# A graph layer's last octets: an addition put ahead of the node statistics, a store cut in two, an earlier flag, and columns copied two octets longer

## The chip, the cores and the metric

The kernel runs on one core of one Trainium2 chip. A core has five engines that work side by side, each on its own queue: TensorE (PE, with its weight loads shown apart as PEld), VectorE (DVE), ScalarE (ACT), GpSimd (POOL) and SyncE (SP). They wait for each other through semaphores; DMA engines move data meanwhile. The metric is the device time of one execution in microseconds (us). A profile is a record of one execution; its span runs from the program's first instruction to its last.

## What is computed

A message passing layer on a graph with 12500 nodes of 64 features and 400000 edges with 16 features, the edges sorted by their destination:

```python
m_in = jnp.concatenate([x[src], x[dst], edge_attr], axis=-1)
h = jax.nn.silu(m_in @ W1 + b1)
messages = jax.nn.silu(h @ W2 + b2)
agg = jax.ops.segment_sum(messages, dst, num_segments=x.shape[0])
node_in = jnp.concatenate([x, agg], axis=-1)
x = _layernorm(x + jax.nn.silu(node_in @ W3 + b3), axis=-1)
```

## The kernel before

The edges are cut into 3125 tiles of 128, and the tiles into 391 **octets** of eight tiles (the last, number 390, has five). A loop over `o` (L759) handles one octet per step, in an order of instructions that is written out by hand for PE, ACT, DVE and SP (`manual_schedule`, L754). POOL runs its own list.

**Where source rows come from.** For most tiles POOL gathers 128 rows of a table with one indirect DMA (`gather`, L448). Some pairs of tiles are built another way, so that POOL issues two gathers fewer per pair: `columns` (L336 to L370) copies 128 columns of a transposed copy of the nodes, one small instruction per column, either on ACT (L367) or on DVE (L369), spread over the three or four octets before the one that uses them. Each group of 16 columns comes after loads of 32 addresses into registers. Which octets get such a pair is planned ahead in `pairs` (L327 to L332): the plan goes over `range(len(octs) - QUIET - 2)` and gives an octet `o + 2` a pair each time an engine has had room for 256 more edges. With `QUIET = 5` ACT builds 113 pairs (14464 columns) and DVE 125 (16000), the last of them used in octets 385 and 383. A third way, rows fetched singly by SP (L397), is not touched.

**One octet.** PE transposes the gathered rows into PSUM (L550), adds the products of copied columns (L553) and of the window and attributes (L554); ACT applies SiLU (L557, `h`); PE multiplies by W2 (L566, L568, `second_layer`); ACT applies SiLU (L572, `m`); PE sums the messages per destination (L581, `add_up`) into one of four places of the PSUM tile `sums`; DVE adds that window to `agg` (L592, `add_window`). [...] The steps at which these happen come from `times` (L727): over the last eight octets (`DRAIN`) `second_layer` is done one step after an octet's first layer, `add_up` two and `add_window` three steps after.

**Nodes.** 25 groups of 512 nodes (the last has 212, on 53 partitions of four nodes) are finished as soon as their sums are complete: products with W3 (L624, L630), SiLU (L636), the sum with x (L642), mean and variance (L647, L648), a square root (L651) and reciprocal (L654) for several groups at once, the division (L660), and the store (L664). The last two groups, `rest` and `rest + 1`, are done at the end.

**The end, in the order of the code.** In the last step but two of the loop's body (`o == NO - 1`, octet 390): `behind` (`add_up(388)`, `second_layer(389)`), the products, SiLU and statistics of group `rest` (L822 to L827), then `limits` (L701 to L718), twelve DVE instructions that check the input's shape, then octet 390's first layer. In step 391 `add_window(388)` comes first (L801), then `add_up(389)` and `second_layer(390)`; in step 392 `add_window(389)` and `add_up(390)`; after the loop `add_window(390)` (L879), the sums and statistics of the last group (L881 to L886), `verdict` (L720 to L725: a small product, a reduction and a conversion, which leave the flag in `badi`), the root, and for both groups division and store (L888 to L893).

**The flag.** After all of this every engine loads the flag `badi` into a register (L106) and branches (L108): if an input's shape is unusual, a general version of the layer is run, else the branch leads past its code. Behind it come semaphore updates that stand in for the part left out (recorded on L108), and the program's end (recorded on L1148): SP waits for all semaphores, each engine drains, and POOL, which gathers the engines' reports, releases them.

Of the kernel before, what the change touches and what calls it, by code (L numbers as in the profile page):

```python
# [20 lines left out]
P = 128  # L21
G = 4
# [19 lines left out]
HALF = 6144  # L42
OVER = 304
TURN = 195
QUIET = 5
DRAIN = 8
LAG = CT * P // 32
AHEADS = 256
# [6 lines left out]
@with_exitstack  # L55
def kernel(
    ctx: ExitStack,
    tc: tile.TileContext,
    x: bass.AP,
    xt: bass.AP,  # L60
    xt2: bass.AP,
    src_c: bass.AP,
    src_row: bass.AP,
    src_pair: bass.AP,
    dst_c: bass.AP,
    dst_row: bass.AP,
    attr_t: bass.AP,
    attr_2: bass.AP,
    base: bass.AP,
    w1: bass.AP,  # L70
    b1: bass.AP,
    w2: bass.AP,
    b2: bass.AP,
    w3: bass.AP,
    b3: bass.AP,
    out: bass.AP,
    edges: int,
):

    nc = tc.nc
    N, D = x.shape

    const = ctx.enter_context(tc.tile_pool(name="const", bufs=1))
    dram = ctx.enter_context(tc.tile_pool(name="dram", bufs=1, space=DRAM))
    pa = dram.tile([N, D], F32, name="pa")
    badi = const.tile([1, 1], I32, name="badi")
    ident = const.tile([P, P], F32, name="ident")
    make_identity(nc, ident)
    identb = const.tile([P, P], BF16, name="identb")  # L100
    nc.vector.tensor_copy(identb, ident)

    with ExitStack() as inner:
        windows(inner, tc, ident, identb, badi, pa, x, xt, xt2, src_c, src_row, src_pair, dst_c, dst_row, attr_t, attr_2, base, w1, b1, w2, b2, w3, b3, out, edges)

    flag = nc.values_load(badi[0:1, 0:1], min_val=0, max_val=4 * P,  # L106
                          skip_runtime_bounds_check_because="a count of partitions")
    with tc.If(flag > 0):  # L108
        general(tc, ident, x, xt, src_c, dst_c, dst_row, attr_t, w1, b1, w2, b2, w3, b3, out, edges)


def windows(ctx, tc, ident, identb, badi, pa, x, xt, xt2, src_c, src_row, src_pair, dst_c, dst_row, attr_t, attr_2, base, w1, b1, w2, b2, w3, b3, out, edges):
    nc = tc.nc
# [4 lines left out]
    NO = base.shape[1]  # L118
# [176 lines left out]
    with tc.tile_pool(name="gat", bufs=AHEAD + 2) as gat, \  # L295
# [32 lines left out]
        for eng in counts:  # L328
            pairs[eng] = []
            for o in range(len(octs) - QUIET - 2):  # L330
                if counts[eng][o] >= 2 * P * (len(pairs[eng]) + 1):
# [121 lines left out]
        def bases(eng, o):  # L453

            n = min(4, NO - o)
            at, least, most = (bi8, 0, 8 * (N - 1)) if eng == ENG.SP else (bi, AADDR, AADDR + 4 * (NA - S))
            _, regs = nc.values_load_multi_w_load_instructions(
                at[0:1, o:o + n], engines=(eng,), min_val=least, max_val=most,
                skip_runtime_bounds_check_because="dst names a node")
            for i in range(n):  # L460
                winreg[eng, o + i] = regs[i]
# [98 lines left out]
        def second_layer(o):  # L560
            c, t0, n, first, last = octs[o]
            n2 = n + n % 2
            k = n2 // 2
            h, eh = made.pop(o)
            p2 = ps2.tile([P, OT, D], F32, name="p2")
            nc.tensor.matmul(p2[:, :n2, :], one3, b2r[:, :n2, :], start=True, stop=False, skip_group_check=True)  # L566
            for i in range(k):
                nc.tensor.matmul(p2[:, 2 * i:2 * i + 2, :].rearrange("p s d -> p (s d)"), h[:, i, :], w2d,  # L568
                                 start=False, stop=(i == k - 1), skip_group_check=True)
            columns(o + 1, ENG.Activation, 1)  # L570
            m = msg.tile([P, OT, D], F32, name="m")
            nc.scalar.activation(m[:, :n2], p2[:, :n2], AF.Silu)  # L572
            made[o] = m, eh

        def add_up(o):
            c, t0, n, first, last = octs[o]
            m, eh = made.pop(o)
            pg = sums[:, o % 4, :]
            for i in range(n):
                s = i % 2  # L580
                nc.tensor.matmul(pg[s * D:(s + 1) * D, :], m[:, i, :], eh[:, i // 2, :, s],  # L581
                                 start=(i < 2), stop=(i >= n - 2), skip_group_check=True)
# [4 lines left out]
        def add_window(o):  # L587
            if o == TURN:
                nc.vector.tensor_copy(agg[:, :OVER], agg[:, HALF:HALF + OVER])
                clear(HALF, NA)  # L590
            a = agg.bitcast(U8)[:, ds((winreg.pop((ENG.DVE, o)) - AADDR).with_bounds(min_val=0, max_val=4 * (NA - S), guaranteed_mod_val=0, out_of_modulus=4), 4 * S)].bitcast(F32)
            nc.vector.tensor_tensor(a, a, sums[:, o % 4, :], op=OP.add)  # L592
# [4 lines left out]
        NG = len(groups)  # L597
        RB = 5
        v = nv.tile([P, 2 * RB, G, D], F32, name="v")
# [26 lines left out]
        def node_sums(q, i):  # L626
            c, n = groups[q]
            a = c if c < HALF else c - HALF
            av = agg[:, a:a + n].rearrange("k (p i) -> k i p", i=G)
            nc.tensor.matmul(nodes[q]["acc"][:n // G, i, :], av[:, i], w3s, start=False, stop=(i == G - 1),  # L630
                             skip_group_check=True)

        def node_silu(q):
            p = groups[q][1] // G
            z = nx.tile([P, G, D], F32, name="z")
            nc.scalar.activation(z[:p], nodes[q]["acc"][:p], AF.Silu)  # L636
            nodes[q]["z"] = z

        def node_add(q):
            p = groups[q][1] // G  # L640
            of = nodes.pop(q)
            nc.vector.tensor_add(v[:p, q % (2 * RB)], of["xa"][:p], of["z"][:p])  # L642

        def node_stats(q, i):
            p = groups[q][1] // G
            st = nx.tile([P, 6], F32, name="st")
            nc.vector.bn_stats(st[:p], v[:p, q % (2 * RB), i, :])  # L647
            nc.vector.bn_aggr(mv[:p, q * G + i, :], st[:p])  # L648
# [7 lines left out]
        def divide(q, i):  # L656
            p = groups[q][1] // G
            vi = v[:p, q % (2 * RB), i, :]
            j = q * G + i
            nc.vector.tensor_scalar(vi, vi, mv[:p, j, 0:1], rstd[:p, j:j + 1], op0=OP.subtract, op1=OP.mult)  # L660

        def store(q):
            c, n = groups[q]
            nc.sync.dma_start(out[c:c + n, :].rearrange("(p i) d -> p i d", i=G), v[:n // G, q % (2 * RB)])  # L664

# [11 lines left out]
        for q in range(rest):  # L679
            o = lead[due[q]] + LAST - 1  # L680
# [10 lines left out]
        for q0, q1 in batches:  # L691
            o = lead[due[q1 - 1]] + LAST + 2 * G
# [27 lines left out]
        def verdict(bad):  # L720
            pc = mis.tile([1, 4], F32, name="mm")
            nc.tensor.matmul(pc, onec, bad, start=True, stop=True)
            bs = nv.tile([1, 1], F32, name="bs")
            nc.vector.tensor_reduce(bs, pc, AX.X, OP.add)
            nc.vector.tensor_copy(badi, bs)  # L725

        def times(lags):  # L727

            at = {}
            for o in range(NO):  # L730
                at.setdefault(o + lags.get(NO - 1 - o, lags[None]), []).append(o)
            return at
# [3 lines left out]
        folds = times({None: LAST, **{k: 3 for k in range(DRAIN)}})  # L736
# [17 lines left out]
        with tc.manual_schedule(engines={ENG.PE, ENG.Activation, ENG.DVE, ENG.SP}):  # L754
# [4 lines left out]
            for o in range(NO + 2):  # L759
# [3 lines left out]
                for k in range(0, NA, XC)[3 * o - 3:3 * o] if o else []:  # L763
                    n = min(XC, NA - k)
# [33 lines left out]
                for b in range(0, NO, 4):  # L798
                    if o == b + (4 if b < NO - DRAIN else 2):
                        bases(ENG.DVE, b)  # L800
                for q in folds.get(o, []):  # L801
                    add_window(q)
                if o == 1:
                    relative(0, CT, SCT)
                for k in range(3 * o - 3, 3 * o) if 1 <= o < 6 else []:
                    if k < 2 * len(parts):
                        c = parts[k // 2]
# [5 lines left out]
                def behind():  # L813
                    for q in adds.get(o, []):
                        add_up(q)
                    for q in seconds.get(o, []):
                        second_layer(q)

                if o == NO - 1:
                    assert NG == rest + 2 and groups[rest][0] + groups[rest][1] + LAG <= (NO - 4) // (CT // OT) * STEP  # L820
                    behind()
                    for i in range(G):  # L822
                        node_sums(rest, i)
                    node_silu(rest)
                    node_add(rest)
                    for i in range(G):
                        node_stats(rest, i)  # L827
                    bad = limits()
# [42 lines left out]
                if o in (NO - 4, NO - 3):  # L871
                    q = rest + (o == NO - 3)
# [4 lines left out]
            for i in range(NO + 2, NO + LAST):  # L877
                for q in folds.get(i, []):
                    add_window(q)  # L879
            assert NO not in todo  # L880
            for i in range(G):  # L881
                node_sums(rest + 1, i)
            node_silu(rest + 1)
            node_add(rest + 1)
            for i in range(G):
                node_stats(rest + 1, i)  # L886
            verdict(bad)
            root(rest, NG)  # L888
            inverse(rest, NG)
            for q in range(rest, NG):  # L890
                for i in range(G):
                    divide(q, i)
                store(q)  # L893


@with_exitstack
# [255 lines left out]
```

## Time and profile before

| | |
|---|---|
| median of 3 runs | 3294.95 us (3292.81 to 3297.97) |
| the profiled execution's own time | 3292.35 us |
| its span | 3290.6 us |
| POOL busy | 2465.6 us (75%), 2505 gathers of L448 from the table and 94 from x |
| ACT busy | 3109.2 us (94%) |
| PE busy | 2486.1 us (76%) |
| DVE busy | 2042.4 us (62%) |
| mean granted TensorE clock | 0.708 |

The profiled execution's time lies 1.75 us above its span. In the rows of the profile a number in front of a unit's name is a time in us; "x16" counts instructions; what stands in brackets or behind a bar is the engine's idle time before the instruction and what ended it. The chain of waits follows the run backwards from its last compute instruction, always to what released it. "issue" means that nothing visible was waited for. The letter q behind an engine (POOLq) marks its sequencer, which waits, branches and issues DMAs.

### The profile page before, as it was taken

Reading aid. Unit: us, or ns where it says so; the run is one execution under the profiler, and the core shown is the slowest. Engines: PE = TensorE matmul, PEld = TensorE weight load, DVE = VectorE, ACT = ScalarE, POOL = GpSimd, SP = SyncE. Lnnn points to the kernel's source line nnn. Section 1 sums busy time; section 2 is a strip of 40 time slices with the busy share of each in tenths; the row PEclk is TensorE's granted clock in tenths of the full one; section 3 lists DMA queues with packets and bytes.
Section 4 is the critical chain, followed back from the end, with each engine's and each line's share of the span. In section 5 each row is a group of like instructions: output and inputs, shape, how many; then the busy total and the mean of one; then the engine's idle time right before and its main releaser. Section 6 shows DMA issues by size and latency. Waiting matters only on the chain. (4 is left out here: it accounts for less than half of the span.)

```text
span 3290.6 us, 88339 instructions
## 1 busy us (share of the span) xinstructions
PE 2486.1 (76%) x15344; PEld 1705.0 (52%) x15344; DVE 2042.4 (62%) x18296; ACT 3109.2 (94%) x15306; POOL 2465.6 (75%) x2607
## 2 busy tenths in 40 slices
PE   7867777777777777767777777777877867777786
PEld 5545555555555545544454554545545545554554
DVE  5566666666666666666666666666666666666652
ACT  2799999999999999999999999999999999999991
POOL 7777777777777777777777777777777777777774
PEclk8787777777667677677767767766666676667666
DMA  7222222222222222221221222222222222222221
GB/s 148 50 41 40 43 41 40 43 41 40 45 44 44 42 42 40 41 43 38 48 46 39 43 41 40 43 43 43 45 41 42 40 44 41 43 44 45 39 42 33
DMA packets 160868, 147.82 MB, mean 45 GB/s; under 512 B 103748, under 2 KB 113718, under 8 KB 159526
## 3 DMA queue, kind: packets, MB, share of 16 engines
q0 software_dynamic: 83168, 85.33, 14.6%
q1 hardware_dynamic: 62624, 47.00, 5.7%
q10 hardware_dynamic: 14502, 9.75, 1.4%
q14 instruction: 447, 3.66, 0.4%
q8 instruction: 127, 2.08, 0.3%
HBM read 135.44 MB, written 6.40 MB: 43 GB/s over the span
## 5 line engine op out<-in xcount | busy, mean ns | idle before, releaser
L448 POOL DMA_INDIRECT ga<-pa,sc x2505 | 2375.6, 948 | 763.9 <-issue 666.0
L367 ACT ACTIVATE cx<-xs,x 128x1 f32 x14464 | 2789.5, 328 | 24.9 <-issue 19.5
L369 DVE TENSOR_TENSOR cx<-xs,x 128x4 uint8 x16000 | 1288.9, 154 | 1095.6 <-issue 1073.7
L581 PEld LDWEIGHTS pg<-eh,m 128*64 128x64 f32 x6250 | 296.8, 184 | 674.5 <-DVE agg L592 344.5
L550 PE MATMUL p<-ident,ga 128*128 128x128 f32 x1253 | 347.1, 364 | 393.7 <-DMA ga<-pa,sc 392.6
L568 PEld LDWEIGHTS p<-w2d,h 128*128 128x128 f32 x3126 | 536.7, 259 | 186.5 <-issue 186.5
L568 PE MATMUL p<-w2d,h 128*128 128x128 f32 x3126 | 632.5, 365 | 0.0
L554 PE MATMUL p<-oh,xw 128*128 128x512 f32 (+1 forms) x758 | 584.6, 866 | 0.0
L581 PE MATMUL pg<-eh,m 128*64 128x48 f32 x6250 | 352.8, 271 | 211.4 <-DVE agg L592 209.1
L550 PEld LDWEIGHTS p<-ident,ga 128*128 128x128 f32 x1253 | 220.4, 186 | 468.4 <-issue 433.2
L557 ACT ACTIVATE h<-p 128x512 f32<-128x512 f32 x391 | 243.1, 622 | 53.5 <-PE p L554 33.1
L515 PE MATMUL ph<-identb,eh 128*96 128x128 bf16 x1563 | 211.9, 276 | 99.9 <-DVE oh L525 96.4
L572 ACT ACTIVATE m<-p 128x512 f32<-128x512 f32 x391 | 242.6, 620 | 41.6 <-PE p L568 40.0
L525 DVE COPY oh<-ph 96x512 f32<-96x512 f32 x391 | 263.1, 673 | 1.9 <-PE ph L515 1.9
L515 PEld LDWEIGHTS <-eh 128*96 128x96 bf16 x1563 | 163.4, 163 | 136.5 <-DVE oh L525 122.4
L566 PE MATMUL p<-b2r,one 3*128 3x512 bf16 x391 | 193.3, 494 | 53.7 <-ACT m L572 53.2
L472 PE MATMUL mm<-w1bb,xr 65*96 65x128 f32 x782 | 221.5, 377 | 6.6 <-DMA xr<-in_xt 4.0
L497 DVE TENSOR_TENSOR eh<-wrow,dc 128x384 f32<-128x384 f32 x392 | 212.5, 542 | 11.3 <-PE wrow L624 6.9
L554 PEld LDWEIGHTS p<-oh,xw 128*128 128x128 f32 x758 | 175.8, 284 | 0.0
L472 PEld LDWEIGHTS mm<-w1bb,xr 65*96 65x96 f32 x782 | 139.9, 230 | 8.1 <-DMA xr<-in_xt 4.2
L553 PE MATMUL p<-cx,w1d 128*128 128x128 f32 x474 | 122.1, 368 | 0.0
L477 DVE TENSOR_TENSOR xw<-mm,mask 96x128 f32<-96x128 f32 x391 | 108.1, 276 | 20.6 <-PE mm L472 18.0
(106 smaller groups left out, 980.1 us busy)
## 6 DMA issues: line engine op xcount, KB each, us to landing
rx<-pa SPq DMA_DIRECT2D x6400, 0.2 KB
ga<-pa,sc POOLq DMA_INDIRECT x2505
oh<-in_attr SPq DMA_DIRECT2D x130, 192.0 KB
xr<-in_xt SPq DMA_DIRECT2D x391, 24.0 KB
cxi<-in_src_pair SPq DMA_DIRECT2D x238, 1.0 KB
xs<-in_xt ACTq DMA_DIRECT2D x6, 512.0 KB
pa<-v ACTq DMA_DIRECT2D x12, 256.0 KB
x<-in_xt ACTq DMA_DIRECT2D x6, 512.0 KB
```

The source lines that it names most:

```text
L367: nc.scalar.activation(cols[key][:, k:k + 1], word(i, xb, XADDR), AF.Identity, bias=word(i + 4, x2b, X2ADDR))
L369: nc.vector.tensor_tensor(t[:, 4 * k:4 * k + 4], at(i, xb, XADDR), at(i + 4, x2b, X2ADDR), op=OP.max)
L448: nc.gpsimd.indirect_dma_start(out=ga[:, i, :], out_offset=None, in_=x if o < RAW else pa[:, :], in_offset=bass.IndirectOffsetOnAxis(ap=sc ...
L472: nc.tensor.matmul(pw[:E, :], winrow[o], w1bb.rearrange("k s m -> k (s m)"), start=True, stop=True)
L515: nc.tensor.matmul(ph[:E, i, :], eh[:, i, :, 1], identb, start=(i == 0), stop=(i == k - 1), skip_group_check=True)
L525: nc.vector.tensor_copy(oh[:E, :], ph[:E, :(n + 1) // 2].rearrange("p i e -> p (i e)"))
L550: nc.tensor.matmul(p1[:, i, :], g2.rearrange("p s d -> p (s d)"), ident, is_transpose=True, start=(i == c), stop=False, skip_group_check=True)
L554: nc.tensor.matmul(p1[:, :k], xw[o % 3], oh, start=False, stop=True, skip_group_check=True)
L557: nc.scalar.activation(h[:, :k], p1[:, :k], AF.Silu)
L568: nc.tensor.matmul(p2[:, 2 * i:2 * i + 2, :].rearrange("p s d -> p (s d)"), h[:, i, :], w2d, start=False, stop=(i == k - 1), skip_group_ch ...
L572: nc.scalar.activation(m[:, :n2], p2[:, :n2], AF.Silu)
L581: nc.tensor.matmul(pg[s * D:(s + 1) * D, :], m[:, i, :], eh[:, i // 2, :, s], start=(i < 2), stop=(i >= n - 2), skip_group_check=True)
```

## The change

It has five parts.

1. `QUIET` goes from 5 to 3, so that the plan covers two more octets. DVE gets one more pair, its 126th, used in octet 386 and copied in the steps 381 to 383; octet 386 has six gathers in place of eight. ACT's pairs stay as they are.
2. `add_window(388)` is taken from the head of step 391 to step 390, between `behind` and the products of group `rest`.
3. `verdict` goes ahead of the last group's sums and statistics.
4. The store of a group is cut at the last multiple of 16 partitions: the last group's 53 partitions go out as 48 and 5. Other groups have 128 and keep one store.
5. The flag is loaded inside `windows`, after the last group's divisions and ahead of its store, and returned.

```diff
-QUIET = 5
+QUIET = 3
...
     with ExitStack() as inner:
-        windows(inner, tc, ident, identb, badi, pa, x, xt, xt2, src_c, src_row, src_pair, dst_c, dst_row, attr_t, attr_2, base, w1, b1, w2, b2, w3, b3, out, edges)
-
-    flag = nc.values_load(badi[0:1, 0:1], min_val=0, max_val=4 * P,
-                          skip_runtime_bounds_check_because="a count of partitions")
+        flag = windows(inner, tc, ident, identb, badi, pa, x, xt, xt2, src_c, src_row, src_pair, dst_c, dst_row, attr_t, attr_2, base, w1, b1, w2, b2, w3, b3, out, edges)
+
...
         def store(q):
             c, n = groups[q]
-            nc.sync.dma_start(out[c:c + n, :].rearrange("(p i) d -> p i d", i=G), v[:n // G, q % (2 * RB)])
+            to, p = out[c:c + n, :].rearrange("(p i) d -> p i d", i=G), n // G
+            for a, b in ((0, p // 16 * 16), (p // 16 * 16, p)):
+                if b > a:
+                    nc.sync.dma_start(to[a:b], v[a:b, q % (2 * RB)])
...
-                for q in folds.get(o, []):
+                for q in folds.get(o, []) if o != NO else []:
                     add_window(q)
...
                     behind()
+                    for q in folds[NO]:
+                        add_window(q)
                     for i in range(G):
                         node_sums(rest, i)
...
             assert NO not in todo
+            verdict(bad)
             for i in range(G):
                 node_sums(rest + 1, i)
...
                 node_stats(rest + 1, i)
-            verdict(bad)
             root(rest, NG)
             inverse(rest, NG)
             for q in range(rest, NG):
                 for i in range(G):
                     divide(q, i)
+                if q == NG - 1:
+                    flag = nc.values_load(badi[0:1, 0:1], min_val=0, max_val=4 * P,
+                                          skip_runtime_bounds_check_because="a count of partitions")
                 store(q)
+    return flag
```

## The prediction

> **What bounds the kernel now.** I read the page first, then the timeline around octets 387 to 390, the chain of waits, and last the control instructions after the last compute.
>
> ```profile
> span 3290.6 us, 88339 instructions
> L448 POOL DMA_INDIRECT ga<-pa,sc x2505 | 2375.6, 948 | 763.9 <-issue 666.0
> ```
> ```profile
> 3238.73 0.45 PE L550 MATMUL p<-ident,ga 128*128 128x128 f32 x1 [1.93 <-DMA ga<-pa,sc]
> 3256.14 0.30 PE L550 MATMUL p<-ident,ga 128*128 128x128 f32 x1 [1.12 <-DMA ga<-pa,sc]
> 3259.87 0.94 POOL L448 DMA_INDIRECT ga<-pa,sc  x1 [0.30 <-issue]
> ```
>
> A gather and its pause take (2375.6 + 763.9) / 2505 = 1.25 us, and the pauses are nearly all POOL's own ("issue"): POOL gathers without a stop until 3260.8. Near the end PE waits for gathers, 1.93 us in octet 387 and 1.12 us in octet 389. So until octet 389's last gather lands POOL bounds the time. Then the bound moves. The chain of waits:
>
> ```profile
> 3264.39 0.43 DVE v L642
> ...
> 3268.74 0.12 DVE agg L592
> 3268.86 0.14 issue
> 3269.00 1.10 PE pg L581 x16
> 3270.09 0.43 PE p L566
> 3270.52 1.59 PE p L568 x6
> 3272.20 0.50 ACT m L572
> 3272.74 0.89 PE pg L581 x10
> 3273.65 0.21 DVE agg L592
> 3273.91 1.12 PE mm L630 x8
> 3275.05 0.39 ACT z L636
> ```
>
> From 3264.39 to 3268.74 it runs through DVE: the sum, the statistics of group rest and the limits, all queued ahead of the addition at 3268.74 (L592, window 388). Only then may PE add up octet 389, and everything behind it follows in a row. The chain ends with the divisions; the rest of the span is control, which I read by line and engine:
>
> ```profile
> 3277.37 0.14 DVE L725 CAST badi<-bs 1x1 int32<-1x1 f32 x1
> ```
> ```profile
> L106 POOLq TENSOR_LOAD <-badi x1: 511/511/511, 3277.5 to 3277.5; - x1
> ```
> ```profile
> L108 POOLq EVENT_SEMAPHORE  x5: 17/43/43, 3281.3 to 3284.2; - x5
> L108 POOLq COMPARE_BRANCH  x1: 53/53/53, 3278.1 to 3278.1; - x1
> L108 POOLq INC_SWDGE_SEM  x1: 1210/1210/1210, 3284.2 to 3284.2; - x1
> ```
> ```profile
> L1148 POOLq DRAIN  x3: 40/107/4230, 3285.5 to 3290.3; - x3
> ```
> ```profile
> SPq L1148 <- PEq L1148: 4.2, 2, 3.7
> SPq L1148 <- DMA ga<-pa,sc: 1.2, 1, 1.2
> ```
>
> POOL loads the flag the moment it is written (3277.51), branches at 3278.1, gets its next instruction at 3281.3, raises its semaphores until 3285.5 and drains for 4.23 us, to 3289.7; at 3290.6 all is over. SP, the last engine beside it, waits 1.2 us for POOL's semaphores and then 3.7 us until POOL lets it go. So the end hangs on POOL's flag: 3290.6 - 3277.5 = 13.1 us from the flag to the end.
>
> **The change part by part.** *Columns.* Two gathers go from octet 386: 2 x 1.25 = **-2.5 us** at POOL. Octets 387 and 389 are gather bound, with PE waiting 1.93 and 1.12 us, so the shift reaches octet 389 whole. The price is 128 copies on DVE in steps 381 to 383:
>
> ```profile
> L369 DVE TENSOR_TENSOR cx<-xs,x 128x4 uint8 x137 | 11.1, 155 | 9.9 <-issue 9.7
> ```
> ```profile
> 3156.00:3181.00 25.00, 20.08 (x136) 14.72 (x134) 15.44 (x150) 25.00 (x126) 18.87 (x20) 0.73 0.20 39
> 3181.00:3206.00 25.00, 16.00 (x98) 9.90 (x98) 6.69 (x30) 21.09 (x102) 18.88 (x20) 0.68 0.20 39
> 3206.00:3256.00 50.00, 40.54 (x262) 28.64 (x261) 12.74 (x46) 10.04 (x15) 37.75 (x40) 0.68 0.22 46
> ```
>
> The first row is the stretch 3156 to 3181: 137 copies take 11.1 us and 9.9 us of pauses for the register loads, 0.153 us each, so 128 take **19.6 us** of DVE's queue. The window rows give the busy time of PE, PEld, DVE, ACT and POOL in this order. In 3181 to 3206, where those steps lie, DVE is busy 6.7 of 25 us: 18.3 are free, and 1.3 us stick out. Behind them stand DVE's `add_window`, `compare_nodes` and `turned`, for which PE waits. A bound from below is 0, from above 19.6 us. I take 0, because the stretch before, 15.44 us of work and 9.9 of pauses on DVE, is just as full and POOL works as steadily in it, and because PE is idle for 50 - 40.54 = 9.5 us between 3206 and 3256, which swallows a lag of 1.3 us. The pair also takes one small index load on SP, one address operation on DVE, and a product (L553) in place of a transpose (L550): nothing of that is on a late path.
>
> *The addition.* It goes ahead of the sum of group rest, into this pause:
>
> ```profile
> 3264.39 0.42 DVE L642 TENSOR_TENSOR v<-xa,z 128x256 f32<-128x256 f32 x1 [6.24 <-ACT z L636]
> ```
> ```profile
> 3260.05 0.67 PE L581 MATMUL pg<-eh,m 128*64 128x48 f32 x16 [0.75 <-ACT m L572]
> 3264.96 0.49 ACT L557 ACTIVATE h<-p 128x384 f32<-128x384 f32 x1 [0.60 <-PE p L554]
> 3269.00 1.10 PE L581 MATMUL pg<-eh,m 128*64 128x48 f32 x16 [4.07 <-DVE agg L592]
> ```
>
> Its input is summed at 3260.72 and DVE is idle for 6.24 us until 3264.39, so the addition itself costs nothing; without that pause it would cost its 0.2 us. What is queued behind it, the sum L642, waits for ACT's z anyway. The products of group rest read `agg` and now wait for it, but they start behind `second_layer(389)`. The 4.07 us wait goes: `add_up(389)` and `second_layer(390)` run under the limits. At the chain's lengths they need h at 3265.45, then 1.59 + 0.1 + 0.50, done by some 3267.7. What is late next is DVE again: `add_window(389)` comes behind the limits, where 388 stood, at 3268.74; then `add_up(390)` starts at 3269.0 in place of 3272.74. **-3.7 us** for all that follows.
>
> *Verdict and flag.* The verdict's product, reduction and conversion now lie between `add_window(390)` (3273.65) and the last group's z (3275.44 at its end), where DVE idles. The addition's 0.21, a reduction and a conversion of 0.14 each and a tenth of waiting make 0.6 us, so the flag is written some 0.6 us behind the start of that addition, not 3277.51 - 3273.65 = 3.86. POOL has nothing else left and loads it at once: **-3.3 us** for POOL's 13.1 us, if these are of fixed length. Their parts (load, branch, semaphores, drain) name no partner in the trace, so I take the length as fixed; if the drain's end hangs on SP, the gain is smaller (rival B).
>
> *Who is last then?* The root, divisions, stores and SP's control shift by the first two terms only.
>
> ```profile
> 3278.91 1.13 SPq L664 DMA_DIRECT2D out<-v  x2
> ```
> ```profile
> L1148 SPq DRAIN  x3: 7/7/13, 3286.2 to 3290.0; - x3
> ```
>
> Without its 1.2 us wait SP would report at 3286.2 - 1.2 = 3285.0, and POOL's release takes 0.9 us more: 3285.9 in the old frame, against POOL's 3290.6 - 3.3 = 3287.3. POOL stays last by 1.4 us. So SP's flag load ahead of the last store and the second store instruction cost nothing: together some 0.4 us more or less on SP, under that 1.4 us. If the cover goes, they cost just that. ACT, DVE and PE load the flag where their lists end, as before. By the same cover the split store brings nothing, although its data land sooner:
>
> ```profile
> GB/s 0 0 0 33 66 66 4 274 180 20 33 25 74 12 49 37 53 25 25 86 25 16 0 0 33 0 33 0 0 0 0 0 0 0 0 0 0 0 0 0
> ```
>
> This is 3278 to 3288 in slices of 0.25 us: the first store passes at 274 and 180 GB/s, the last trickles at about 25 GB/s until some 3283.5. [...]
>
> *Sum.* -2.5 - 3.7 - 3.3 = **-9.5 us**. The span goes from 3290.6 to 3281.1, the profiled execution's own time from 3292.35 to 3282.9. That execution is 2.6 us below the median of 3294.95, so against the median I get **3285.4**.
>
> **The rivals.** *B: POOL's long drain waits for the others.* It ends 3.5 us behind SP's report (3286.2 to 3289.7). Against it: POOL started it before SP had reported. Then SP's chain decides: 3285.0 + 3.5 + 0.9 = 3289.4, less 6.2: -7.4 us, 3287.5.
>
> *C: the tail on half a clock.*
>
> ```profile
> 3243.00:3253.00 10.00, 10.00 (x55) 7.79 (x54) 2.71 (x11) 1.19 (x2) 7.56 (x9) 0.57 0.16 26
> 3253.00:3260.00 7.00, 5.19 (x46) 3.44 (x44) 1.65 (x6) 1.79 (x3) 5.17 (x7) 1.00 0.25 64
> ```
> ```profile
> 3242.38 2.08 PE L568 MATMUL p<-w2d,h 128*128 128x128 f32 x8
> 3260.97 1.16 PE L568 MATMUL p<-w2d,h 128*128 128x128 f32 x8
> ```
>
> The granted clock was 0.57 up to 3253 and 1.00 behind it, just before the tail's chain, and eight products of L568 take 2.08 us on the low clock, 1.16 on the full. If the rise comes later against the work, two such blocks cost 0.9 each, two of L581 0.4 each, and the other products of that chain, slowed in the same ratio, by estimate 1.7 together: +4.3, so -5.2 us, 3289.8. For it: the moved gathers shift the work against the clock's steps. Against it: PE is as busy before the tail as it was. [...]
>
> *D: the extra copies eat the gathers' gain.* DVE's 1.3 us grows, PE reaches octet 389 2.5 us late: -7.0, 3287.9. For it: DVE and ACT are full in the stretch before.
>
> *E, slower: the copies gate PE.* If next to none of the 19.6 us on DVE is hidden, PE falls back by that in steps 381 to 383, regains its 9.5 us of idle time and starts octet 389's tail 10.1 us later than now; the other terms give back 7.0: +3.1, **3298.0**. It decides from 16.5 us of exposed copies on. Against it: 18.3 us of free DVE time.
>
> That the change does not do what it says would show as a flag that POOL does not load sooner; that is -6.2 and lies between D and C.
>
> **How the numbers follow.** Forecast 0.52, B 0.16, C 0.15, D 0.12, E 0.05. Runs of before spread by 2.6 us around their median, and SP's bound alone would allow 1.4 us more gain. The range goes from 3285.4 - 1.4 - 2.6 = 3281.4 up to C with 1.5 us of that spread, 3291.3; E and the edges, some 0.15, stay out. 0.2% is 6.6 us, about what a measurement of this kernel can tell from no change. Faster by more: the forecast nearly whole (0.48) and two thirds of B and D (0.19), so 0.67; same: their rest, and C, 0.28; slower: E, 0.05.
>
> **What would show it.** Right: 2503 gathers on L448 and the last one 2.5 us sooner; 16128 copies on L369; no wait of PE L581 for DVE L592 near 4 us; `add_up(390)` right behind the limits; the flag's conversion about 0.6 us behind the last addition, POOL's load at once, and some 13 us from there to the end, the drain still 4.2 us. Wrong: a POOL drain that grows when it starts sooner (B); L568 at 2.08 us for eight in octet 389's tail (C); PE waiting for DVE at L581 or L554 in octets 382 to 386 (D, E).

## The result, and the profile after

Eight runs of the changed kernel have a median of **3282.97 us** (3281.24 to 3286.59), against 3294.66 us (3292.81 to 3297.97) in eight runs of the kernel before. The ratio is 0.9965, with a 95% interval of 0.9954 to 0.9976: 11.7 us less by the medians, and more than the 0.2% that can be told from no change. The profiled execution took 3282.35 us. These are the page's span and its two groups of gathers and DVE columns:

```profile
span 3280.6 us, 88479 instructions
...
L446 POOL DMA_INDIRECT ga<-pa,sc x2503 | 2375.1, 949 | 763.4 <-issue 654.8
...
L367 DVE TENSOR_TENSOR cx<-xs,x 128x4 uint8 x16128 | 1300.1, 154 | 1100.6 <-issue 1075.5
```

Two gathers are gone and 128 copies have come, at the same price each as before. Lines of the octets and nodes are two lower than before (L581 is now L579), those behind the new store one or more higher (L704 is L705, L1148 is L1155). The timeline of the changed kernel (start, busy time, engine, line):

```profile
3254.34 0.30 PE L548 MATMUL p<-ident,ga 128*128 128x128 f32 x1 [1.24 <-DMA ga<-pa,sc]
3254.48 1.02 PE L552 MATMUL p<-oh,xw 128*128 128x512 f32 x2
3255.44 0.67 PE L579 MATMUL pg<-eh,m 128*64 128x48 f32 x16
...
3258.07 0.94 POOL L446 DMA_INDIRECT ga<-pa,sc  x1 [0.30 <-issue]
3258.26 0.67 PE L579 MATMUL pg<-eh,m 128*64 128x48 f32 x16 [0.75 <-ACT m L570]
3258.98 0.20 DVE L590 TENSOR_TENSOR agg<-agg,pg 128x48 f32 x1 [2.62 <-PE pg L579]
...
3263.06 0.67 PE L579 MATMUL pg<-eh,m 128*64 128x48 f32 x16
...
3266.87 0.19 DVE L590 TENSOR_TENSOR agg<-agg,pg 128x48 f32 x1
3267.21 0.85 PE L579 MATMUL pg<-eh,m 128*64 128x48 f32 x10 [2.35 <-DVE agg L590]
3268.10 0.20 DVE L590 TENSOR_TENSOR agg<-agg,pg 128x48 f32 x1 [1.03 <-PE pg L579]
...
3268.40 0.14 DVE L726 CAST badi<-bs 1x1 int32<-1x1 f32 x1
```

Read it from top to bottom. PE still waits for a gather in octet 389 (1.24 us). The addition of window 388 comes at 3258.98, in DVE's pause, and `add_up(389)` starts at 3263.06 with no wait for DVE. The 4.07 us wait is gone. Behind the limits stands `add_window(389)` at 3266.87, and `add_up(390)` waits 2.35 us for that one. The flag is ready 0.45 us behind the start of the last addition.

The control instructions of the changed kernel by line and engine (count, shortest, median and longest duration in ns, then first and last start in us):

```profile
L897 POOLq TENSOR_LOAD <-badi x1: 511/511/511, 3268.6 to 3268.6; - x1
```
```profile
L106 POOLq EVENT_SEMAPHORE  x5: 17/43/43, 3271.8 to 3274.0; - x5
L106 POOLq COMPARE_BRANCH  x1: 53/53/53, 3269.2 to 3269.2; - x1
L106 PEldq COMPARE_BRANCH  x1: 3910/3910/3910, 3269.2 to 3269.2; - x1
L106 ACTq COMPARE_BRANCH  x1: 58/58/58, 3272.1 to 3272.1; - x1
L106 DVEq COMPARE_BRANCH  x1: 72/72/72, 3272.8 to 3272.8; - x1
...
L106 POOLq INC_SWDGE_SEM  x1: 1170/1170/1170, 3274.1 to 3274.1; - x1
```
```profile
L1155 POOLq DRAIN  x3: 40/107/4067, 3275.3 to 3280.3; - x3
L1155 SPq DRAIN  x3: 7/7/13, 3279.7 to 3280.0; - x3
```

POOL loads the flag at once, at 3268.6, starts its long drain at 3275.3 and has ended it at 3279.4. SP reports at 3279.7 (the first start in its drain row, and so in every kernel below), 0.3 us later, and 0.9 us behind that the span ends. POOL and SP now end together.

Cut at four points, the two profiled executions compare like this (us; each number a difference of two starts, or of a start and the span, in the timelines):

| from, to | before | after | difference |
|---|---|---|---|
| start to last gather of the table | 3259.87 | 3258.07 | -1.80 |
| to `add_up(388)` | 0.18 | 0.19 | 0.0 |
| to `add_window(390)` | 13.60 | 9.84 | -3.76 |
| to the end | 16.92 | 12.46 | -4.46 |
| sum | 3290.57 | 3280.56 | -10.0 |

The first, third and fourth difference stand for the three terms of the prediction, in its order. The last gather is only a marker: it serves octet 390, whose transposes start at 3261.98 without a wait. The one that PE waits for, octet 389's last, is the sixth from the end. It starts at 3251.83 where it was 3253.62, sooner by the same 1.8 us.

### The profile page after: what moved, and what is told of

Same layout as the page of the kernel before. It is cut to its first block, busy times and chain, and to the rows that moved or that the text cites. A ratio compares the mean times of both kernels' runs of the same rounds, so it can differ in the third digit from the quotient of the medians.

```text
span 3280.6 us, 88479 instructions
## 1 busy us (share of the span) xinstructions
PE 2488.6 (76%) x15345; PEld 1725.1 (53%) x15345; DVE 2054.0 (63%) x18425; ACT 3107.3 (95%) x15306; POOL 2465.0 (75%) x2605
## 3 DMA queue, kind: packets, MB, share of 16 engines
q0 software_dynamic: 83104, 85.26, 11.7%
## 5 line engine op out<-in xcount | busy, mean ns | idle before, releaser
L579 PEld LDWEIGHTS pg<-eh,m 128*64 128x64 f32 x6250 | 297.7, 184 | 722.6 <-DVE agg L590 422.3
L566 PE MATMUL p<-w2d,h 128*128 128x128 f32 x3126 | 640.1, 368 | 0.0
L548 PE MATMUL p<-ident,ga 128*128 128x128 f32 x1252 | 337.9, 366 | 331.1 <-DMA ga<-pa,sc 329.6
L579 PE MATMUL pg<-eh,m 128*64 128x48 f32 x6250 | 353.7, 271 | 264.7 <-DVE agg L590 263.6
```

The source lines that it names most:

```text
L548: nc.tensor.matmul(p1[:, i, :], g2.rearrange("p s d -> p (s d)"), ident, is_transpose=True, start=(i == c), stop=False, skip_group_check=True)
```

## The experiments

My theory at this point: three terms that add up, the gathers, the addition and the flag; the split store and SP bring nothing; and the tail is shorter than predicted because POOL's way from the flag to its drain's end is no fixed length. The rivals: the store's sooner landing brings part of the tail; the drain waits for partners (B); PE's clock or DVE's copies eat the gathers (C, D).

**Each part alone.** Four kernels, each the kernel before with one part of the change, on one chip, where the kernel before took 3295.14 us. The edits, in this order:

```diff
-QUIET = 5
+QUIET = 3
```
```diff
-                for q in folds.get(o, []):
+                for q in folds.get(o, []) if o != NO else []:
...
                     behind()
+                    for q in folds[NO]:
+                        add_window(q)
```
```diff
...
             assert NO not in todo
+            verdict(bad)
...
-            verdict(bad)
             root(rest, NG)
...
+                if q == NG - 1:
+                    flag = nc.values_load(badi[0:1, 0:1], min_val=0, max_val=4 * P,
...
                 store(q)
+    return flag
```
```diff
-            nc.sync.dma_start(out[c:c + n, :].rearrange("(p i) d -> p i d", i=G), v[:n // G, q % (2 * RB)])
+            to, p = out[c:c + n, :].rearrange("(p i) d -> p i d", i=G), n // G
+            for a, b in ((0, p // 16 * 16), (p // 16 * 16, p)):
+                if b > a:
+                    nc.sync.dma_start(to[a:b], v[a:b, q % (2 * RB)])
```

> The kernel before with only the copied columns two octets longer (QUIET = 3). Theory (POOL bounds until the last octets): the last gather starts 2 x 1.25 = 2.5 us sooner and the whole tail behind it keeps its length of 3290.6 - 3259.9 = 30.7 us, so -2.5 us. Rival (the copies on DVE cost PE what the gathers give): last gather sooner, but PE no longer waits for gathers in octet 389, the tail longer by up to 2.5 us, 0 in all. Rival (the copies gate PE): +10 us, with PE waiting for DVE in octets 382 to 386.

> The kernel before with only add_window(388) ahead of the sum of group rest. Theory: the last addition on DVE starts 3.7 us closer to the last gather (before: 3273.65 - 3259.87 = 13.8, now 10.1), and everything behind it, POOL's flag included, follows: -3.7 us. Rival (something else lies just under the wait that goes, such as octet 390's second layer): less than 2 us.

> The kernel before with only the verdict ahead of the last group's sums and the flag's load ahead of the last store. The flag is written 0.45 us behind the start of the last addition in place of 3.86. Theory as predicted (POOL's way from the flag to its drain's end has a fixed length of 12.2 us and decides): -3.4 us. Rival 1 (that way is 10.9 us, as in the changed kernel, because fewer engines branch and fetch instructions at the same time): POOL is done 4.7 us sooner and SP reports about as late, so -4.3 to -4.7 us. Rival 2 (the drain ends 3.5 us behind SP's report): -2 us, and a drain longer than 4.2 us.

> The kernel before with only the last store cut into 48 and 5 partitions. Theory: SP branches later by some 0.9 us (0.82 + 0.36 for the two issues in the changed kernel, 0.25 for the one before), hidden behind POOL, which is last here: 0 us, not over +0.3. Rival (the end hangs on the landing of the last data): -2 us, with SP's first semaphore update behind the branch as much sooner.

Measured, with the stretches of the profiled execution in us:

| kernel | median | ratio, interval | to `add_up(388)` from last gather | to `add_window(390)` | to the end |
|---|---|---|---|---|---|
| columns alone | 3293.03 | 0.999, 0.9981 to 1.0 | 2.17 | 13.61 | 16.27 |
| addition alone | 3291.22 | 0.9985, 0.9976 to 0.9994 | 0.26 | 9.51 | 16.55 |
| flag alone | 3290.70 | 0.9983, 0.9974 to 0.9992 | 0.14 | 13.59 | 12.82 |
| split alone | 3294.79 | 1.0, 0.9991 to 1.0009 | 0.28 | 13.61 | 16.39 |

By medians the parts bring 2.1, 3.9, 4.4 and 0.35 us, 10.8 together, where the whole brings 11.7. The addition and the flag are shown by times. The columns' interval touches 1, so their 2.1 us fits two gathers of 1.25 us but isn't shown by times. Where the gathers bound the loop, the last one starts anywhere from 3257.9 to 3264.6 in the five profiles with 2503 for the table, the later ones below included, and from 3259.9 to 3264.4 in the four with 2505, so its start in one pair of profiles can't size the term either. Counted from a fixed gather well ahead of octet 386 it can be sized. These are the starts of the 2441st, before and after:

```profile
3179.95 0.94 POOL L448 DMA_INDIRECT ga<-pa,sc  x1 [0.30 <-issue]
```
```profile
3180.64 0.95 POOL L446 DMA_INDIRECT ga<-pa,sc  x1 [0.30 <-issue]
```

From there to the start of the last gather it is 79.92 us before (3259.87) and 77.43 after (3258.07). The four profiles with 2505 have 79.90 to 80.13 us, the five with 2503 77.42 to 77.58. So POOL is done 2.5 us sooner, as forecast; 0.7 us of that was lost ahead of this point in the pair above. Whether all of it reaches the end hangs on PE.

The addition alone does what the table says, as the timeline of that kernel shows:

```profile
3264.63 0.67 PE L581 MATMUL pg<-eh,m 128*64 128x48 f32 x16 [0.75 <-ACT m L572]
...
3273.59 0.52 PE L581 MATMUL pg<-eh,m 128*64 128x48 f32 x10 [2.35 <-DVE agg L592]
3274.14 0.20 DVE L592 TENSOR_TENSOR agg<-agg,pg 128x48 f32 x1 [0.70 <-PE pg L581]
```

The next wait is the 2.35 us behind the limits that the whole change has too. Of the 4.09 us by which its stretch is shorter than before (13.60 to 9.51), 0.35 are not the change's: the ten products of `add_up(390)` took 0.52 us in this execution, at a granted clock of 1.00, and 0.87 in the profile of the kernel before, at 0.50.

The columns' profile holds a surprise. Its window and timeline:

```profile
3250.00:3260.00 10.00, 10.00 (x47) 6.05 (x46) 3.33 (x12) 1.19 (x2) 7.56 (x9) 0.50 0.18 44
```
```profile
3239.97 0.45 PE L550 MATMUL p<-ident,ga 128*128 128x128 f32 x1 [1.61 <-DMA ga<-pa,sc]
...
3257.34 1.06 PE L550 MATMUL p<-ident,ga 128*128 128x128 f32 x4
...
3260.96 0.94 POOL L448 DMA_INDIRECT ga<-pa,sc  x1 [0.31 <-issue]
...
3263.13 0.67 PE L581 MATMUL pg<-eh,m 128*64 128x48 f32 x16 [0.75 <-ACT m L572]
```

The granted clock was 0.50 through 3250 to 3260, where it was 1.00 from 3253 in the kernel before. PE was busy all of those 10 us, its transposes at 3257.34 wait for no gather, and `add_up(388)` starts 2.17 us behind the last gather in place of 0.18. So in this one execution rival C ate about 2 us, most of the gathers' gain. The copies (D) were not the cause: they end at 3209.5, and at 3239.97 PE still waits 1.61 us for a gather, so it was not late then.

In the flag-alone kernel the end hangs on POOL. Its control instructions:

```profile
L1150 POOLq DRAIN  x3: 40/107/4230, 3282.8 to 3287.6; - x3
L1150 SPq DRAIN  x3: 7/7/13, 3286.4 to 3287.3; - x3
```

POOL drains for 4.23 us from 3282.75 to 3286.98; SP reports at 3286.4. SP's report comes 3.7 us behind the drain's start here, 0.7 us behind it in the kernel before (3286.2 against 3285.5), and the drain has the same 4.230 us in both. Rival B is refuted: the drain doesn't wait for SP. Of the expectations the fixed length failed: 4.4 us by medians and 4.1 by the stretch, where 3.4 was expected. POOL's way from the flag to its drain's end took 11.53 us here, against 12.21 in the kernel before.

**Verdict late, and no split.** Two kernels, each the changed kernel with one part undone. The first puts the verdict back behind the last group's statistics, the second stores in one piece:

```diff
-            verdict(bad)
             for i in range(G):
                 node_sums(rest + 1, i)
...
+            verdict(bad)
             root(rest, NG)
```
```diff
-            for a, b in ((0, p // 16 * 16), (p // 16 * 16, p)):
-                if b > a:
-                    nc.sync.dma_start(to[a:b], v[a:b, q % (2 * RB)])
+            nc.sync.dma_start(out[c:c + n, :].rearrange("(p i) d -> p i d", i=G), v[:n // G, q % (2 * RB)])
```

> The changed kernel with the verdict back behind the last group's statistics; the flag's load stays ahead of the last store. The flag is then written 3.9 us behind the start of the last addition again (changed kernel: 0.45), and PE, POOL, ACT and DVE branch nearly together. Theory A (POOL's way from flag to drain's end is of fixed length, 10.9 us as in the changed kernel): POOL is last again and the stretch from the last addition to the end is 3.9 + 10.9 + 0.8 = 15.6 us, against 12.5: +3.1 us to the changed kernel. Theory B (it grows when the engines fetch instructions together): over 11.5 us from flag to drain's end, +3.8 us and more. Theory C (SP and its stores set the end anyway): +0.3 us.

> The changed kernel with the last store in one piece again. In the changed kernel SP reports at 3279.73, 0.33 us behind POOL's drain, and its two last issues take 0.82 and 0.36 us. Theory (the two issues only delay SP's branch): SP branches some 0.9 us sooner, POOL's drain is last, 0.2 to 0.4 us less from the last addition to the end (12.5 to about 12.1), nothing that the times can show. Rival (the landing counts): the 53 rows land some 3.6 us behind their issue, SP has to wait for them: 0.5 us more or above.

These two and the next two ran on a chip where every kernel took some 4955 us, the one before 4961.61. From 1000 to 1500 us SP issued 678 row fetches in the no-split kernel there, 1042 in the changed kernel above. POOL waited for PE in that time:

```profile
POOL ga L446 <- PE p L548: 139.2, 25, 10.0
```

In the changed kernel this wait is 2.7 us. So on that chip the gathers don't bound the loop, and two fewer can gain nothing; that SP's slow issue is what bounds it is likely but not shown. I compare only the stretches of the tail, which lie behind the last row fetch (4908.8 in the no-split kernel).

With the verdict late, the stretch from `add_window(390)` to the end is 16.42 us, and the flag comes 3.86 us behind the addition, as before the change. Without the split the stretch is 12.42 us on that chip (12.46 with it in the changed kernel), so the late verdict costs 4.0 us. POOL's way from the flag to its drain's end is 11.71 us, not the 10.9 of a fixed length. The control instructions without the split:

```profile
L1152 POOLq DRAIN  x3: 40/107/4067, 4943.7 to 4948.4; - x3
L1152 SPq DRAIN  x3: 7/7/13, 4947.5 to 4948.1; - x3
```

Here POOL's drain ends at 4947.8, 0.3 us behind SP's report; with the split SP is 0.3 us behind POOL. What the split costs SP is seen in the issues: the two parts took 0.82 and 0.36 us in the changed kernel, 1.20 and 0.32 in the split-alone kernel, and one store of 53 rows 0.25 to 0.28. That lies beside POOL's drain. The data do land sooner with it: the last packet of the store starts 8.1 us behind the last addition in the changed kernel, 9.8 in the no-split one. There SP waits 0.7 us for that landing ahead of its report, so the split saves this wait and spends it on the dearer issue. It brings nothing either way, alone or in the whole, though 0.2 to 0.4 us were expected back without it, so the sooner landing, the rival for the tail, is out.

Now the length of POOL's way. The control instructions of the late-verdict kernel:

```profile
L106 ACTq COMPARE_BRANCH  x1: 58/58/58, 4938.8 to 4938.8; - x1
L106 POOLq COMPARE_BRANCH  x1: 53/53/53, 4939.0 to 4939.0; - x1
L106 PEldq COMPARE_BRANCH  x1: 4007/4007/4007, 4939.1 to 4939.1; - x1
L106 DVEq COMPARE_BRANCH  x1: 72/72/72, 4939.2 to 4939.2; - x1
...
L106 POOLq INC_SWDGE_SEM  x1: 1170/1170/1170, 4944.9 to 4944.9; - x1
```

The four engines branch within 0.4 us, and POOL needs 5.83 us (unrounded) from its branch to INC_SWDGE_SEM. In the changed kernel only PE branches with POOL; ACT and DVE follow 3.0 and 3.6 us later, and POOL needs 4.97 us. Over the profiles: 5.59 to 6.13 us in the five where four engines branch together (before, columns, addition, split, late verdict), 4.90 to 5.45 us in eight with the early verdict; the ninth of these, the last kernel below, has 2.98. That POOL's way is longer in that company is shown, and undoing the verdict alone brings it back; that the engines hinder each other in getting their next instructions is what I infer.

The way has two pauses: one from the branch to the first of the five semaphore updates, 2.56 to 3.16 us, and one among these updates. The second is 2.37 to 2.64 us in the five profiles of the late verdict and 1.98 to 2.31 in the eight. In the last kernel below it is absent, which is all that its 2.98 us differ by:

```profile
L106 POOLq EVENT_SEMAPHORE  x5: 17/43/43, 3264.8 to 3265.2; - x5
```

The updates follow each other within 0.4 us here, within 2.2 us in the changed kernel (3271.8 to 3274.0). What POOL waits for in that pause, and why it is absent once, stays open.

**The limits ahead too.** The wait of 2.35 us suggests a next step: the twelve instructions of the limits read inputs only, and can run in DVE's pause before group `rest`'s sum. And a further one: the verdict behind octet 390's first layer, so that the flag is ready before the last addition, with the last two groups' stores on ACT, so that SP is free to load the flag early. Both start from the changed kernel, the second from the first:

```diff
...
                         add_window(q)
+                    bad = limits()
                     for i in range(G):
                         node_sums(rest, i)
...
                         node_stats(rest, i)
-                    bad = limits()
```
```diff
-        def store(q):
+        def store(q, eng=nc.sync):
...
                     first_layer(o)
+                if o == NO - 1:
+                    verdict(bad)
...
-            verdict(bad)
...
-                store(q)
+                store(q, nc.scalar)
```

> The changed kernel with the twelve instructions of the limits moved from behind group rest's statistics to ahead of its products, into the 3.4 us in which DVE waits for that group's z. Theory (after the change the next late thing is the queue of DVE ahead of add_window(389)): add_up(390) then waits for its own messages (ready at 3265.45) and not for DVE: the last addition starts 1.5 to 1.7 us closer to the last gather (changed kernel: 10.0 us behind it), -1.6 us to the changed kernel. Rival (PE's own order is as late): under 0.5 us.

> The limits moved as in the run before, the verdict behind the last octet's first layer, and the last two stores issued by ACT, so that POOL and SP load the flag, branch and raise their semaphores under the last group's work. Theory (what remains behind the last store is the issuing engine's branch and instruction fetch of 2.6 us and the barrier of 0.9): ACT is the last to report, POOL's drain is over before; -1.6 us from the limits and about -1 us at the end, -2.6 us to the changed kernel. Rival (the data's landing sets the end): SP waits at its semaphores, less than 0.5 us gained at the end.

Medians were 4959.32 us with the verdict late (ratio 0.9992, 0.9983 to 1.0001), 4953.91 without the split (0.9983, 0.9974 to 0.9992), 4953.23 with the limits first (0.9982, 0.9973 to 0.9991) and 4951.75 for the last (0.9971, 0.9961 to 0.9981). With the limits first it is 7.83 us in place of 9.83 (no split) from `add_up(388)` to `add_window(390)`; 0.3 of these 2.0 us are again the ten products (0.55 us in place of 0.85). In the last kernel the stretch behind that is 10.88 in place of 12.46, but the one ahead of it 10.66, so of the 2.6 us expected 0.8 is left in this execution. One of its windows shows why:

```profile
4931.00:4937.00 6.00, 6.00 (x32) 5.00 (x28) 3.34 (x16) 0.98 (x2) 0.00 (x0) 0.50 0.00 0
```

The granted clock was 0.50 there, in the midst of the tail: rival C once more, in this one execution.

**Again where the gathers bound the loop.** The same two, the changed kernel itself, and a fourth that adds `QUIET = 1` to the last, which covers two octets more and takes four more gathers away. Here the kernel before took 3296.26 us:

> The changed kernel once more, beside the three runs that follow, since in the second set of runs SyncE issued the row fetches so slowly that it bounded the whole loop (the kernel before took 4961.61 us there). All theories: -10 to -12 us to the kernel before; from the sum of octet 388 to the last addition 9.8 us, from there to the end 12.4 to 12.5 us, POOL 10.8 to 11.6 us from the flag to its drain's end.

> The limits ahead of group rest's products, where the loop is bounded by POOL. Theory (DVE's queue ahead of add_window(389) is late): 7.8 us from the sum of octet 388 to the last addition in place of 9.8, and -2 us to the changed kernel on the same chip; the end from the last addition on as there, 12.4 us. Rival: the order saves nothing in time because PE or ACT turn late: under 0.5 us.

> The limits moved, an early verdict, the last stores from ACT. Theory: 10.9 us from the last addition to the end in place of 12.4, and 7.8 us from the sum of octet 388 to the last addition; -3.5 us to the changed kernel on the same chip. Rival (an earlier verdict takes PE's and DVE's time in the chain): the stretch to the last addition over 8.3 us, less than 3 us gained.

> As the run before, and the copied columns two octets longer again (QUIET = 1): a pair of ACT in octet 388 and one of DVE in octet 389, four gathers fewer. Theory as for the first two octets (POOL bounds, copies hide): 4 x 1.25 = 5 us less to the run before. Rival (the idle time on ACT, DVE and PE between octets 384 and 389 is what let PE catch up, and the copies now reach into it): the sum of octet 388 no longer starts right behind the last gather (0.2 us) but 2 us or more later, so under 3 us gained.

| kernel | median | ratio, interval | to `add_up(388)` from last gather | to `add_window(390)` | to the end |
|---|---|---|---|---|---|
| the change again | 3283.01 | 0.9965, 0.9952 to 0.9979 | 0.13 | 9.50 | 12.35 |
| limits first | 3281.62 | 0.9957, 0.9943 to 0.997 | 0.44 | 7.83 | 12.64 |
| and verdict sooner, stores on ACT | 3282.10 | 0.9957, 0.9943 to 0.997 | 1.65 | 7.95 | 10.87 |
| and `QUIET = 1` | 3278.92 | 0.9953, 0.9939 to 0.9966 | 2.87 | 7.95 | 10.92 |

The ratio is estimated from the runs, and isn't the quotient of the medians. The change repeats its ratio; that its median comes within 0.04 us of the first is luck, for its five runs go from 3281.67 to 3286.08. With the limits first, DVE leaves the path; the chain of waits in that kernel runs through PE and ACT up to the last addition:

```profile
3269.89 0.60 PE pg L579 x16
...
3270.76 0.88 PE p L566 x6
...
3271.72 0.50 ACT m L570
3272.26 0.56 PE pg L579 x10
3272.85 0.22 DVE agg L590
```

The stretches are 1.7 us and then 1.8 us shorter. The medians follow by 1.4 us and then not at all, and all four intervals overlap. Against the expectations, 2 us for the limits became 1.4 and 3.5 us for both steps became 0.9. In the profile of the third, PE reached `add_up(388)` 1.65 us behind the last gather. Its timeline:

```profile
3256.41 1.92 PE L552 MATMUL p<-oh,xw 128*128 128x512 f32 x2
3258.26 1.09 PE L579 MATMUL pg<-eh,m 128*64 128x48 f32 x16
```

In the changed kernel such groups, at 3254.48 and 3255.44, take 1.02 and 0.67 us. The granted clock from 3250 to 3260 was 0.83 here and 1.00 there, so part of the shorter tail was given back ahead of it. Whether that is so in its other runs, the times don't tell. The fourth is the fastest by its median; its timeline:

```profile
3252.38 0.94 POOL L446 DMA_INDIRECT ga<-pa,sc  x1 [0.30 <-issue]
...
3255.25 0.67 PE L579 MATMUL pg<-eh,m 128*64 128x48 f32 x16 [0.75 <-ACT m L570]
```

PE comes 2.87 us behind the last gather, and its transposes of octet 389 wait for none: gathers no longer bound the end there, and part of the four gathers is spent. By medians they bring 3.2 us where 5 were expected, near what the rival on record for that run had (under 3). No version is shown to beat the change.

## Why the prediction was right

The sign, the mechanism and the range held: 3285.4 us was forecast within 3281.4 to 3291.3, and 3282.97 came. Point by point:

**Columns, -2.5.** 2503 gathers and 16128 copies, as said. Counted from a fixed gather POOL is done 2.5 us sooner in every profile where gathers bound the loop. The starts of the last gather in the pair show 1.8 us, the part alone 2.1 us by medians; neither is finer than the spread of a run. The 19.6 us of copies were hidden in the changed kernel, as I took them. The changed kernel's window of those steps, and its gather-fed transposes from 3210 to 3256 with the same group of the kernel before behind them:

```profile
3181.00:3206.00 25.00, 18.41 (x121) 11.88 (x121) 15.29 (x147) 22.02 (x105) 18.88 (x21) 0.73 0.17 39
```
```profile
L548 PE MATMUL p<-ident,ga 128*128 128x128 f32 x19 | 5.3, 337 | 13.1 <-DMA ga<-pa,sc 13.1
```
```profile
L550 PE MATMUL p<-ident,ga 128*128 128x128 f32 x19 | 5.2, 352 | 7.7 <-DMA ga<-pa,sc 7.7
```

DVE is busy 15.29 us where it was 6.69, POOL as busy as ever, and behind that stretch PE waits for gathers longer than before, 13.1 us against 7.7. Part of that longer wait may be the clock, which was 0.80 from 3206 to 3256 in this profile and 0.68 before. But in octet 389 PE still waits, 1.24 us here and 1.5 when the kernel was run again, so it isn't late from the copies: D and E are out for the change. C was real: the granted clock was 0.50 from 3250 to 3260 in the profile of the columns alone, and in those of the kernel with the stores on ACT 0.50 from 4931 to 4937 and 0.83 from 3250 to 3260. In the changed kernel it was 1.00 from 3250 to 3260, and in both profiles of the change PE reached `add_up(388)` within 0.2 us of the last gather's start. What sets the times of the clock's steps, no run shows; that the rise could come later was my estimate.

**Addition, -3.7.** 3.76 us in the whole; alone 4.09 by stretches, 3.74 without the faster products, and 3.9 by medians. What is late next is `add_window(389)` behind the limits, as named. That an octet's sums wait for the window addition of the octet before, though the two use different places of `sums`, is seen in the waits: 4.07 us at `add_up(389)` before the change, 2.35 us at `add_up(390)` after it, both for L592 (now L590).

**Verdict and flag, -3.3: the mis-sized term.** The stretch behind the last addition shrank by 4.46 us. The flag came 0.45 us behind the addition, not 0.6, which gives 3.41 in place of 3.3. The other 1.05 us lie behind the flag: "if these are of fixed length" was the step that failed. From the flag written to the end of POOL's drain it is 12.21 us before and 10.85 after: 1.16 less from branch to INC_SWDGE_SEM (6.13 to 4.97), 0.04 in that, and 0.16 in the drain. The last two are the two gathers' doing, not the flag's: the flag alone leaves them at 1.21 and 4.23 us. The 1.16 is large by luck of the pair: 6.13 is the longest of its five profiles, and the means of the five and the eight, 5.82 and 5.15, are 0.7 apart. So POOL doesn't stay last by 1.4 us: SP takes over and holds back 0.3 us. With POOL's way shorter by 1.36, the cover that I counted on was used up, and SP's own chain ended 0.3 us behind POOL in the changed kernel and under 0.1 us when it was run again.

**The split store and SP's flag load.** Nothing, as said, though SP's issue of the split, 1.18 us in place of 0.25, cost more than the 0.4 us that I gave it; POOL's end hid it but for those tenths. The "about 25 GB/s" of the last store holds for its end: from 3282.2 to 3283.4 it moves 29 packets of 1 KB, one by one and 0.042 us apart. Over all, the slices of that row also hold other packets, and their mean from 3280.25 to 3283.5 is 37. That the split's data land sooner is shown by no row of the kernel before, but by the runs: all 53 packets start within 0.5 us in the changed kernel (3275.66 to 3276.16), and the last packet comes 8.1 us behind the last addition, against 9.8 without the split.

By the sum, -9.5 predicted stands against -10.0 in the profiles and -11.7 in the medians. That the first two are so close is in part luck, for the gathers' 0.7 us less and the flag's 1.2 us more nearly cancel. The missing 1.7 us between the last two lie in the choice of executions: the profiled one before was 2.3 us below its median of eight, the one after 0.6 us below.

## What to carry to other kernels

When a step is held up behind another engine's queue, look for the pause in that queue ahead of the point where its input is ready, and count what is late next; here that gave the gain to 0.1 us. A length behind a wait that names no partner, such as the control instructions after a branch, may still change when other engines arrive at the same time (here 5.82 us in the mean where four engines branch together, 5.15 with the early verdict): bound it by what was seen, not as a constant. And a term that is under a run's spread, such as two gathers of 1.25 us in a 3290 us kernel, can't be shown by times of the whole; counted from a fixed instruction ahead of the change, it can be shown at its engine.

## What the runs showed of the hardware

POOL's long drain at the program's end follows the number of gathers. The rows of the kernel with the stores on ACT and of the one with `QUIET = 1`, and, above, those of the flag alone:

```profile
L1156 POOLq DRAIN  x3: 40/107/4067, 3275.0 to 3280.0; - x3
```
```profile
L1156 POOLq DRAIN  x3: 40/107/3740, 3266.4 to 3273.8; - x3
```

With the 94 gathers from x it is 4.230 us for 2599 gathers, 4.067 for 2597 and 3.740 for 2593, the same in every kernel of one count: 82 ns for each gather. INC_SWDGE_SEM goes the same way: 1.210, 1.170 and 1.095 us, 19 ns for each. In the kernel with the stores on ACT, ACT and SP report 0.3 us behind the drain's end, and the drain is as long as the others of its count. Why a drain should know the count of all gathers, no run tells. Beyond the three counts the rule isn't tried.

POOL's way from its branch to INC_SWDGE_SEM varied from 2.98 to 6.13 us, longest with four engines branching at once, as told above: a pause of 2.56 to 3.16 us behind the branch and, in all profiles but one, a second of 1.98 to 2.64 us. PE's branch itself took 3.35 to 4.01 us.

The DMA records hold reads on queues marked "instruction", nine or ten of 8 KB and two of 16 KB in the tail of each profile. The first 16 KB read starts 0.9 to 1.0 us behind PE's branch. It took 1.43 to 1.55 us in the five profiles where four engines branch together, with three reads of 8 KB begun by 1.6 us behind that branch, and 0.94 to 1.33 us in the eight others with the second pause, where one or two were. That fits engines that hinder each other. But the last kernel had three such reads and a 16 KB read of 1.41 us, and POOL's way was its shortest; so the cause isn't settled by it.
